# A graph network on one core: from one pair of graphs at a time to three stages with buffers of their own

## The chip, the core and the metric

One core of a Trainium2 chip. Times are device microseconds (us) of one whole execution, the median of several. "Clock" is the mean granted TensorE clock of an execution, 1.0 being full. A program on one core is compared in rounds with the kernel before on the same chip. In profile lines PE is TensorE (matrix products and transposes) and PEld its loads of weights; DVE is VectorE, ACT ScalarE and POOL GpSimd, which do the rest. SBUF is the memory that they work in, PSUM the one that takes TensorE's results, which the kernels hand out in tiles called banks (a wide tile counts as two).

## The reference, cut to what matters

64 graphs of 256 nodes with 256 features, fp32, with an integer adjacency matrix each. Four layers follow one another, and each ends with `x = layernorm(x + layer(x))`:

```
layer 0  masked attention, 8 heads of 32:  x1 = LN(x + softmax(mask(q k^T)) v Wo^T; ln1)
         feed-forward 256 -> 1024 -> 256:  x2 = LN(x1 + relu(x1 W1^T + b1) W2^T + b2; ln2)
layer 1  graph attention: h = x W^T, e = leaky(f_i + g_j), masked softmax, out = softmax(e) h + bias
layer 2  graph attention as before, then elu
layer 3  two convolutions: elu(x w_root + b + (mask^T x / degree) w_rel), twice
```

## The kernel before

It takes the graphs two at a time: 32 pairs, one after another. A pair has six norms: one after attention, two in a row after the feed-forward, one after each graph attention, one after the convolutions. Each norm goes from VectorE (statistics) to GpSimd (add epsilon, power of -0.5) and back to VectorE. The result of the power is called the root below. All big values share a few tags ("res", "xT") and the four PSUM banks of "mm":

```python
    ps_s = ctx.enter_context(tc.tile_pool(name="ps_s", bufs=2, space=PSUM))
    ps_m = ctx.enter_context(tc.tile_pool(name="ps_m", bufs=4, space=PSUM))
    ...
    def layer_norm(y, g=None, b=None):
        ...
        for i in range(NT):
            nc.vector.bn_stats(st[:, i, :], y[:, i, :])
            nc.vector.bn_aggr(mv[:, i, :], st[:, i, :])
        rstd = small.tile([P, NT], F32, tag="rstd", name="rstd")
        nc.gpsimd.tensor_scalar(rstd, mv[:, :, 1], EPS, None, op0=ALU.add)
        nc.gpsimd.tensor_tensor(rstd, rstd, neghalf, op=ALU.pow)
        o = tok(F32, "res", RES)
        for i in range(NT):
            mean, r = mv[:, i, 0:1], rstd[:, i : i + 1]
            if g is None:
                nc.vector.tensor_scalar(o[:, i, :], y[:, i, :], mean, r, op0=ALU.subtract, op1=ALU.mult)
            else:
                ...
        return o
    ...
    with tc.tile_pool(name="work", bufs=2) as pools["work"]:
        loaded = {0: load(x_view[0], adj_view[0])}
        for g in range(B // 2):
            ...
            xt = layer0(xt, attention(transposed(xt), am))
            xt = layer1(xt, gm)
            xt = layer2(xt, gm)
            xt = layer3(xt, adj)
            nc.sync.dma_start(out_view[g], xt)
```

## Time and profile before

| | before |
|---|---|
| median of 3 runs | 5842.55 us (5841.83 to 5842.78) |
| steady time of one pair | 180.9 us |
| TensorE busy, clock | 68%, 0.794 |
| VectorE, GpSimd, ScalarE busy | 45%, 21%, 18% |

The profile lines are shown in the prediction. One more view is used from here on, a **ledger of TensorE's time**, worked out from the trace. All matmul records of 16 steady pairs are sorted by their start. From one start to the next, the usual distance of that form at full clock is "work" (for example 0.429 us for 512 columns), time in which no record runs is "empty", and what remains is excess, booked by the clock at that moment. I read excess at full clock mostly as waiting that the record does not show as a gap. Before, a pair's 180.9 us are 90.3 of work, 56.9 empty, 27.3 of excess at half clock and 6.4 of excess at full clock.

### The profile page before, as it was taken

The numbers are of one execution on the slowest core, as the hardware profiler recorded it, in microseconds if no ns is written. First come the engines' busy times: TensorE is split into PE (matmuls) and PEld (weight loads), VectorE is DVE, ScalarE is ACT, GpSimd is POOL, SyncE is SP. The second block draws the span as 40 slices with busy tenths as digits, with TensorE's granted clock in tenths as the row PEclk, the third lists the DMA queues.
The fourth block names the chain that finished last, engine by engine and source line by source line (L and its number), as shares of the span: only waits on it lengthen the run. The fifth ranks groups of instructions, "written<-read, shape, count | busy, mean of one in ns | idle before, by whom it ended". The sixth has DMA issues, their size and how long they took to land. (4 is left out here: it accounts for less than half of the span.)

```text
span 5841.5 us, 44000 instructions
## 1 busy us (share of the span) xinstructions
PE 3973.4 (68%) x17170; PEld 2521.4 (43%) x17170; DVE 2625.8 (45%) x5370; ACT 1074.5 (18%) x1953; POOL 1255.0 (21%) x1012
## 2 busy tenths in 40 slices
PE   5766677666776667666677666777666776667766
PEld 3444444444444444444444444444444444444443
DVE  3444444544445434454444443444434445444453
ACT  1211112111121111111111211112111121111211
POOL 2221222212222122221122211222212222122221
PEclk8877788777887778877788777887777887778877
DMA  2000000000000000000000000000000000000000
GB/s 67 8 11 4 11 11 8 11 7 9 11 8 11 11 4 11 8 11 11 4 11 11 8 11 4 11 11 8 11 4 11 11 8 11 4 11 11 4 4 4
DMA packets 55542, 59.78 MB, mean 10 GB/s; under 512 B 2016, under 2 KB 54496, under 8 KB 55328
## 3 DMA queue, kind: packets, MB, share of 16 engines
q1 hardware_dynamic: 50688, 50.34, 2.8%
q10 hardware_dynamic: 4032, 5.24, 0.3%
q8 instruction: 137, 2.24, 0.2%
q0 software_dynamic: 608, 1.32, 0.1%
q14 instruction: 77, 0.63, 0.0%
HBM read 40.12 MB, written 16.78 MB: 10 GB/s over the span
## 5 line engine op out<-in xcount | busy, mean ns | idle before, releaser
L179 PE MATMUL mm<-ident,res 128*128 128x128 f32 x1280 | 331.9, 431 | 1123.5 <-DVE res L199 869.5
L179 PEld LDWEIGHTS mm<-ident,res 128*128 128x128 f32 x1280 | 237.6, 212 | 1205.7 <-issue 652.7
L379 PE MATMUL mm<-h,e 128*128 128x259 f32 x1024 | 418.0, 594 | 341.0 <-DVE e L371 341.0
L183 ACT COPY xT<-mm 128x512 f32<-128x512 f32 x192 | 112.3, 585 | 2504.2 <-PE mm L179 2504.2
L432 PE MATMUL mm<-cw,xT 128*128 128x512 f32 x1024 | 529.3, 675 | 4.6
L260 PE MATMUL mm<-xT,W1T 128*128 128x512 f32 x1024 | 496.7, 647 | 18.3 <-DVE xT L181 18.3
L244 DVE TENSOR_TENSOR res<-mm,res 128x512 f32<-128x512 f32 x128 | 86.5, 675 | 925.5 <-PE mm L242 925.5
L379 PEld LDWEIGHTS mm<-h,e 128*128 128x128 f32 x1024 | 313.0, 313 | 432.3 <-DVE e L371 353.2
L242 PE MATMUL mm<-W2T,hid 128*128 128x256 f32 x2048 | 447.2, 379 | 0.0
L242 PEld LDWEIGHTS mm<-W2T,hid 128*128 128x128 f32 x2048 | 389.1, 190 | 66.5 <-issue 15.3
L276 PE MATMUL mm<-gw,xT 128*128 128x258 f32 x1024 | 357.2, 523 | 23.0 <-DVE xT L181 18.3
L190 DVE BATCH_NORM_STATS2 st<-res 128x6 f32<-128x256 f32 x768 | 297.5, 412 | 159.3 <-POOL res L265 78.4
L338 ACT ACTIVATE p<-s 128x1024 f32<-128x1024 f32 x256 | 259.6, 1019 | 576.0 <-PE s L333 548.3
L333 PE MATMUL s<-qk 32*128 32x256 f32 x2048 | 286.3, 496 | 102.1 <-ACT p L338 64.5
L193 POOL TENSOR_SCALAR rstd<-mv 128x4 f32<-128x4 f32 x192 | 53.5, 279 | 1396.4 <-DVE mv L191 1396.4
L341 POOL TENSOR_TENSOR p<-p,am 128x1024 f32<-128x1024 f32 x128 | 305.2, 2384 | 202.5 <-ACT p L338 202.5
L432 PEld LDWEIGHTS mm<-cw,xT 128*128 128x128 f32 x1024 | 220.8, 223 | 283.5 <-issue 222.4
L352 DVE RECIPROCAL inv<-mm 128x512 f32<-128x512 f32 x64 | 214.9, 3358 | 273.5 <-PE mm L349 273.5
L260 PEld LDWEIGHTS mm<-xT,W1T 128*128 128x128 f32 x1024 | 212.9, 212 | 288.3 <-issue 257.3
L276 PEld LDWEIGHTS mm<-gw,xT 128*128 128x128 f32 x1024 | 272.6, 274 | 107.1 <-DVE xT L181 48.5
L199 DVE TENSOR_SCALAR res<-res,mv,rstd 128x256 f32<-128x256 f32 x512 | 239.7, 530 | 169.2 <-POOL rstd L194 167.8
L451 POOL TENSOR_TENSOR res<-res 128x1024 f32<-128x1024 f32 x32 | 75.1, 2347 | 1075.0 <-DVE res L296 1075.0
(112 smaller groups left out, 5858.8 us busy)
## 6 DMA issues: line engine op xcount, KB each, us to landing
x<-in_x_dram SPq DMA_DIRECT2D x32, 512.0 KB, 3.8
adj<-in_adj_dram SPq DMA_DIRECT2D x32, 512.0 KB, 3.8
out_dram<-res SPq DMA_DIRECT2D x32, 512.0 KB, 2.9
W1T<-in_W1T_dram ACTq DMA_DIRECT2D x1, 1024.0 KB, 8.6
W2T<-in_W2T_dram ACTq DMA_DIRECT2D x1, 1024.0 KB, 18.5
WqkvT<-in_WqkvT_dram ACTq DMA_DIRECT2D x1, 768.0 KB, 4.6
cw<-in_w_root_dram ACTq DMA_DIRECT2D x2, 256.0 KB, 8.4
cw<-in_w_rel_dram ACTq DMA_DIRECT2D x2, 256.0 KB, 8.7
```

The costliest lines, as they stand in the source:

```text
L179: nc.tensor.transpose(pt[:, i * P : (i + 1) * P], xt[:, i, kb * P : (kb + 1) * P], ident)
L190: nc.vector.bn_stats(st[:, i, :], y[:, i, :])
L199: nc.vector.tensor_scalar(o[:, i, :], y[:, i, :], mean, r, op0=ALU.subtract, op1=ALU.mult)
L242: nc.tensor.matmul(po[:, i, :], lhsT=lhs(c)[:, tile_i], rhs=rhs(c), start=(c == 0), stop=(c == n - 1))
L260: nc.tensor.matmul(ph, lhsT=w1[:, kb, f * P : (f + 1) * P], rhs=x1T[:, kb, :], start=(kb == 0), stop=(kb == KB - 1))
L276: nc.tensor.matmul(ph, lhsT=xT[:, kb, i * P : (i + 1) * P], rhs=w[:, kb, :], start=(kb == 0), stop=(kb == KB - 1))
L333: nc.tensor.matmul(s[r // 2][:, r % 2, hg, :], lhsT=qk[rows_r, KB + hg, n * P : (n + 1) * P], rhs=qk[rows_r, hg, queries], start=True, sto ...
L338: nc.scalar.activation(pu, s[u], AF.Exp, accum_out=sums[:, u : u + 1])
L341: eng.tensor_tensor(flat, flat, am[:, n, None, :].to_broadcast([P, 4, N]), op=ALU.mult)
L352: nc.vector.reciprocal(inv, pd)
L379: nc.tensor.matmul(po, lhsT=e[:, 2 * b + kt, i * P : (i + 1) * P], rhs=h[:, 2 * b + kt, :], start=(kt == 0), stop=(kt == 1))
L432: nc.tensor.matmul(po, lhsT=hT[:, kb, n * P : (n + 1) * P], rhs=w[:, kb, :], start=(kb == 0), stop=(kb == KB - 1))
```

## The change

The intent: three pairs under way at once. The work is cut into three stages (attention with its norm; feed-forward and first graph attention; second graph attention and convolutions), each with SBUF tags and PSUM banks of its own, so that the holes of one pair can take the matmuls of two others. To make room, norms and row biases work in place, and x and adj are loaded again where a later stage needs them. Some checks and a few passes were moved or merged. The core of the diff, cut:

```diff
-    ps_s = ctx.enter_context(tc.tile_pool(name="ps_s", bufs=2, space=PSUM))
-    ps_m = ctx.enter_context(tc.tile_pool(name="ps_m", bufs=4, space=PSUM))
+    ps = {
+        "wide": ctx.enter_context(tc.tile_pool(name="ps_wide", bufs=2, space=PSUM)),
+        "a": ctx.enter_context(tc.tile_pool(name="ps_a", bufs=2, space=PSUM)),
+        "b": ctx.enter_context(tc.tile_pool(name="ps_b", bufs=2, space=PSUM)),
+    }
...
+    s1, s2, s3, gen = Stage("a_", "wide"), Stage("b_", "a"), Stage("c_", "b"), Stage("g_", "a")
...
+    def add_row(xt, row):
+        nc.gpsimd.tensor_tensor(xt, xt, over_tiles(row), op=ALU.add)
...
-        o = tok(F32, "res", RES)
         for i in range(NT):
-            mean, r = mv[:, i, 0:1], rstd[:, i : i + 1]
+            yi, mean, r = y[:, i, :], mv[:, i, 0:1], rstd[:, i : i + 1]
             if g is None:
-                nc.vector.tensor_scalar(o[:, i, :], y[:, i, :], mean, r, op0=ALU.subtract, op1=ALU.mult)
+                nc.vector.tensor_scalar(yi, yi, mean, r, op0=ALU.subtract, op1=ALU.mult)
...
-        x2 = layer_norm(y, ln2g, ln2b)
-        nc.gpsimd.tensor_tensor(x2, x2, xt, op=ALU.add)
-        return layer_norm(x2)
+        layer_norm(st, y, ln2g, lambda i: xt[:, i, :])
+        layer_norm(st, y)
...
+    def stage1(g, kept):
+        xt, adj = kept.pop("in")
+        am, kept["gm"] = masks(s1, adj)
+        xT = transposed(s1, xt)
+        add_row(xt, bo)
+        kept["x"] = attention_end(s1, xt, attention(s1, xT, am, g))
+
+    def stage2(g, kept):
+        xt = load(s2, x_view[g], F32, "x")
+        kept["x"] = layer1(s2, feed_forward(s2, kept["x"], xt), kept["gm"], 2 * g)
+
+    def stage3(g, kept):
+        adj = load(s3, adj_view[g], I32, "adj")
+        xt = layer2(s3, kept["x"], kept["gm"], 2 * g + 1)
+        nc.sync.dma_start(out_view[g], layer3(s3, xt, *relation(s3, adj, g)))
...
+        for step in range(G + 2):
+            if step >= 2:
+                stage3(step - 2, pairs.pop(step - 2))
+            if 1 <= step <= G:
+                stage2(step - 1, pairs[step - 1])
+            if step + 1 < G:
+                fetch(step + 1)
+            if step < G:
+                stage1(step, pairs[step])
```

## The prediction

> **What bounds the kernel now.** I read the page's busy shares first, then the timeline of one pair of graphs, then a table of windows that cuts that pair into the stages the change uses.
>
> The page's first two parts (busy time and share by engine; the span in 40 slices):
>
> ```profile
> PE 3973.4 (68%) x17170; PEld 2521.4 (43%) x17170; DVE 2625.8 (45%) x5370; ACT 1074.5 (18%) x1953; POOL 1255.0 (21%) x1012
> ...
> PEclk8877788777887778877788777887777887778877
> DMA  2000000000000000000000000000000000000000
> ```
>
> No engine is full. TensorE is busiest, at 68%, and its granted clock is about 0.8 all along (mean 0.794). DMA is near zero after the first loads, so bandwidth is no limit. A kernel in which nothing is full waits on its own chain.
>
> The timeline of TensorE for one pair (start us, length us, line, in brackets the idle time before and its releaser):
>
> ```profile
> 2071.47 3.57 PE L242 MATMUL mm<-WoT,ctxT 128*128 128x256 f32 x8 [2.30 <-DVE ctxT L353]
> 2079.03 2.31 PE L179 MATMUL mm<-ident,res 128*128 128x128 f32 x8 [3.99 <-DVE res L202]
> 2081.91 15.49 PE L260 MATMUL mm<-xT,W1T 128*128 128x512 f32 x32 [0.57 <-DVE xT L181]
> 2097.23 13.98 PE L242 MATMUL mm<-W2T,hid 128*128 128x256 f32 x64
> 2122.90 2.19 PE L179 MATMUL mm<-ident,res 128*128 128x128 f32 x8 [11.69 <-DVE res L199]
> ...
> 2137.15 6.62 PE L379 MATMUL mm<-h,e 128*128 128x259 f32 x16 [5.32 <-DVE e L371]
> 2147.20 1.94 PE L179 MATMUL mm<-ident,res 128*128 128x128 f32 x8 [3.44 <-DVE res L199]
> ...
> 2161.33 6.47 PE L379 MATMUL mm<-h,e 128*128 128x259 f32 x16 [5.32 <-DVE e L371]
> 2167.64 0.34 PE L417 MATMUL mm<-ones_b,rel_b 128*128 128x1 bf16 x8
> 2180.10 2.10 PE L179 MATMUL mm<-ident,res 128*128 128x128 f32 x8 [12.11 <-DVE res L199]
> ```
>
> Every norm (L199, L202) and every softmax of the graph attention (L371) leaves TensorE empty for 3 to 12 us, and no matmul of another pair stands in these holes. The first matmuls of the next pair come only after the last convolution of this one: all pairs draw from the same tags (the four banks of "mm", "res", "xT"), and these are handed out in program order. So the period is one pair's latency: the second convolution's transposes start at 2015.27 and at 2196.14, 180.9 us apart, and 32 x 180.9 = 5788 leaves 53 us for start and end.
>
> The same pair by stage (attention; its output product and norm; feed-forward and first graph attention; second graph attention and the convolutions; last row, the whole period):
>
> ```profile
> core 0: us, PE busy (x) PEld busy (x) DVE busy (x) ACT busy (x) POOL busy (x), PEclk, DMA share, GB/s
> 2027.60:2071.40 43.80, 34.64 (x250) 19.18 (x248) 30.88 (x38) 11.39 (x20) 19.29 (x14) 0.88 0.08 25
> 2071.50:2079.00 7.50, 3.54 (x8) 2.50 (x9) 4.22 (x14) 0.00 (x0) 1.53 (x3) 0.73 0.00 0
> 2079.00:2147.10 68.10, 46.71 (x148) 31.46 (x148) 21.48 (x60) 10.04 (x17) 11.09 (x10) 0.80 0.03 8
> 2147.20:2208.60 61.40, 39.21 (x134) 25.66 (x135) 25.27 (x60) 12.11 (x24) 6.87 (x5) 0.73 0.00 1
> 2027.60:2208.40 180.80, 123.93 (x538) 78.71 (x536) 81.85 (x168) 33.54 (x61) 38.88 (x31) 0.79 0.03 9
> ```
>
> Of a period TensorE is busy 124 us and empty 57 us; VectorE is busy 82. The new stages are 51, 68 and 61 us long when alone.
>
> [...]
> - [...] Starts of 512-column matmuls (L260) are 429 ns apart where the granted clock is 1.0 and 853 ns where it is 0.5, and the transposes that follow the norms (L179 on res) nearly all run at 0.5, 214 ns apart, against 109 for the transposes of x, which follow a full stretch.
> - [...] the 128x256 norm step (L199) took 407 ns on average with GpSimd idle and 2440 ns in the 31 cases where it mostly lay beside a GpSimd instruction; the head mask (L341) took 1.22 us at least and 2.20 us beside GpSimd.
> - [...]
>
> **The change, part by part.**
>
> *Own buffers and banks for each stage (the main part).* Attention works in two 4 KB PSUM tiles, the other two stages in two banks each, and each has its own SBUF tags. The holes of one pair can then take matmuls of two others. TensorE's work at full clock, from the start-to-start times in the trace at clock 1.0, per pair: 48 fp32 transposes x 109 ns = 5.2; 8 bf16 ones x 56 and 8 broadcasts x 108 = 1.3; L218 16 x 429 = 6.9; L229 16 x 216 = 3.5; L333 in 16 groups of four at 232 = 3.7; L349 in 32 groups of four at 217 = 6.9; WoT 16 x 216 = 3.5; W1 32 x 429 = 13.7; W2 64 x 216 = 13.8; L276 32 x 217 = 6.9; L379 32 x 221 = 7.1; L432 32 x 429 = 13.7; L443 32 x 120 = 3.8; degrees 0.2. Sum **90 us**, against 124 busy today: the 34 us between are the half clock and the tails of bursts. If TensorE never idles, 32 pairs cost 2890 us.
>
> How full it gets: one chain alone at full clock has 90 us of TensorE and 57 us without it, so its idle share is 57/147 = 0.39. If three chains were idle independently, all three would be so 0.39^3 = 6% of the time: 96 us a pair. Counting only two as able to cover for each other (stages hand over to each other[...]) gives 15% idle: **106 us**. I choose the second, and add the next item.
>
> *More VectorE beside GpSimd.* GpSimd's long SBUF-reading instructions come to about 26 us per pair (six 128x1024 adds of 2.34 to 2.69, four mask products of 2.38, two of 1.27). [...] Some 47 VectorE instructions per pair can be caught, each for half of about 2.3 us: 47 x 0.23 x 1.15 = 12 us, of which I put half on the path: **6 us**. Together 112 us.
>
> *Operations removed from VectorE.* Bias of v folded into the output bias (L231, 1.3 us per pair, now a ScalarE copy of about 0.6 us x 2); the squares and maxima of the checks (L361, L362, 0.7) to GpSimd (about 0.44 x 2); three passes over "other" (L410 to L412, 2.1) become one of about 1.2; the fp32r compare (L406), 2.43 us beside GpSimd's compare (L408, 2.81 us, now gone), perhaps 0.7. Saved: 1.3 + 0.7 + 0.9 + 1.7, some 4.6 us, so VectorE falls from 82 to about 77 before new blocking, near 89 after it. GpSimd falls from 39 to about 35. None sets the period while TensorE needs 90.
>
> *Norms and biases in place.* The residual add between the two norms (L265, 2.34 us plus its 2.45 us wait) leaves the chain, since x + bias is made earlier. As chain time this is covered by other pairs anyway; what it buys is SBUF room.
>
> *Added:* x and adj are loaded once more, 1 MB per pair, at a DMA share of 0.03: hidden. *Start and end:* 53 us as now, then the first steps with one stage (51) and two (about 70), the last with two (75) and one (61): 310 us, around 30 full steps.
>
> Sum: 30 x 112.5 + 310 = 3685, **say 3690 us**.
>
> **Rivals.**
> 1. *VectorE becomes the bound.* 77 us of work plus 12 or more of blocking is as much as TensorE's 90[...]. For it: the 2440 ns case above. [...] It would give 120 to 130 us a pair: 3900 to 4200.
> 2. *Banks bind.* Attention had eight banks and gets four, of which scores take all four at once; a stage with two banks can run only one group ahead. For it: in the convolution ScalarE and VectorE need 0.37 + 0.43 + 0.41 us per bank after a 1.7 us product. Against: that is shorter than the product, and other stages fill in. If wrong, holes of 1 to 3 us return between groups, and the time goes to about 4000.
> 3. *Nearly perfect overlap.* 96 us a pair and a clock of 1.0: about 3190. For it: long FFN and convolution bursts need almost nothing from VectorE. Against: fixed order, and two engines at over 80% together.
> 4. *No overlap gained* (a shared resource still in program order): about 5700. The distinct tags speak against it.
>
> **Range and chances.** 3380 to 4150: from 102 us a pair (3370) to 128 (4150). Faster by over 2% 0.97, within 2% 0.02, slower 0.01.
>
> **What would show it.** Right: TensorE busy over 85% with the clock over 0.93; transposes after norms at some 110 ns instead of 214; the steady period 105 to 120 us; VectorE's and GpSimd's shares rising to about 70% and 30%; L199 and L202 longer on average than 530 and 482 ns. Wrong: a clock still near 0.8 (holes remain), VectorE over 85% busy (rival 1), or TensorE waiting chiefly for evacuations (rival 2).

## The result

| | before | after |
|---|---|---|
| median | 5842.59 us | 4516.38 us (4493.25 to 4520.36, 4 runs) |
| ratio | | 0.7722 (95% interval 0.77 to 0.7744) |
| steady time of one pair | 180.9 us | 136.7 us (one of 130 to 137, one of 138 to 143 in turn) |
| TensorE busy, clock | 68%, 0.794 | 84%, 0.877 |
| ledger: work / empty / half clock / full-clock excess | 90.3 / 56.9 / 27.3 / 6.4 | 91.0 / 19.9 / 15.9 / 10.0 |

Ratios, here and below, are the mean time of one kernel's runs over that of the other's runs of the same rounds, so not quite the ratio of the medians. Executions over 1.5% slower than the fastest of the same kernel are left out of the means. The change is a large gain, but 826 us short of the 3690 predicted, and outside the range.

The page of the changed kernel (busy time and share by engine; the clock in 40 slices, in tenths):

```profile
PE 3769.8 (84%) x17174; PEld 2277.5 (51%) x17174; DVE 2498.4 (56%) x5148; ACT 1097.4 (24%) x2017; POOL 1114.0 (25%) x915
...
PEclk8888889889898988888988898898888988899887
```

TensorE is fuller, VectorE is not: 56%, where about 70% was forecast. The clock rose only to 0.877. The table of windows shows how two successive pairs go through (four phases, then the whole double period):

```profile
core 0: us, PE busy (x) PEld busy (x) DVE busy (x) ACT busy (x) POOL busy (x), PEclk, DMA share, GB/s
2006.70:2050.50 43.80, 43.80 (x165) 27.91 (x164) 22.12 (x53) 10.64 (x19) 3.61 (x3) 1.00 0.12 36
2050.50:2132.70 82.20, 65.67 (x351) 39.06 (x350) 48.13 (x89) 21.13 (x41) 27.14 (x21) 0.83 0.04 13
2132.70:2186.70 54.00, 51.64 (x191) 32.03 (x190) 26.53 (x65) 13.55 (x23) 8.10 (x8) 0.97 0.06 20
2186.70:2273.00 86.30, 67.95 (x356) 40.75 (x355) 51.81 (x94) 21.70 (x41) 26.44 (x22) 0.82 0.06 19
2006.70:2280.90 274.20, 234.38 (x1070) 142.41 (x1069) 153.62 (x317) 67.61 (x125) 68.86 (x56) 0.87 0.06 20
```

The overlap is not even. In the short phases (44 and 54 us) the feed-forward of one pair and the convolutions of the pair before fill TensorE, at clock 1.00 and 0.97. In the long ones (82 and 86 us) the two graph attentions of a pair run beside the attention of the next, full of norms and softmaxes; TensorE is busy 80% and 79% of them, at clock 0.83 and 0.82. A pair takes from its attention's start at 2050.9 to the end of its convolutions near 2320, about 270 us: two periods, so on average two pairs are under way, not three.

Inside a long phase, holes stand ahead of the transposes that follow a norm (timeline of TensorE; start, length, in brackets the idle time before and what ended it):

```profile
2060.69 1.01 PE L227 MATMUL ps_a<-ident,b_x 128*128 128x128 f32 x4 [2.72 <-DVE b_x L247]
...
2085.79 1.12 PE L227 MATMUL ps_b<-ident,b_x 128*128 128x128 f32 x3 [4.23 <-DVE b_x L247]
...
2124.46 1.54 PE L227 MATMUL ps_a<-ident,a_x 128*128 128x128 f32 x6 [3.84 <-DVE a_x L250]
2126.78 3.82 PE L421 MATMUL ps_b<-c_h,c_e 128*128 128x259 f32 x8 [0.78 <-DVE c_e L413]
```

L247 and L250 are the last steps of norms. These holes stood there before too (35.2 us a pair ahead of such transposes, 3.8 of it behind an elu and not a norm; now 10.4); they shrank, but in a kernel with three stages one expects them filled. The clock shows it too: of the transposes that follow a norm 73% still start at half clock (before, 1272 of the 1280 transposes of res, L179, did), where the prediction's sign of being right was 110 ns instead of 214.

Two smaller forecasts can be checked at once in the groups by line, after:

```profile
L247 DVE TENSOR_SCALAR b_x<-b_x,b_mv,b_rstd 128x256 f32<-128x256 f32 x256 | 150.4, 649 | 113.2 <-POOL b_rstd L243 113.2
...
L247 DVE TENSOR_SCALAR c_x<-c_x,c_mv,c_rstd 128x256 f32<-128x256 f32 x128 | 44.2, 408 | 64.2 <-POOL c_rstd L243 64.2
...
L452 DVE TENSOR_SCALAR c_rel<-c_adj 128x1024 fp32r<-128x1024 int32 x32 | 21.8, 683 | 0.0
```

The same norm step takes 649 ns on average where it often lies beside a GpSimd instruction (45 of these 256 lie for over half their length beside one and take 1788 ns, 185 lie beside none and take 406 at the median), and 408 ns where it does not: the slowing beside GpSimd that the prediction had read from the kernel before (407 against 2440 ns for this step; "blocking" below) is there. Not every instruction shows it: in the kernel before, the copy L181 out of PSUM took 692 ns on average in the 64 cases beside a GpSimd instruction and 689 in the 128 others. The fp32r compare fell from 2428 to 683 ns, as predicted.

### The profile page after: what moved, and what is told of

It reads as the page before. It is cut to its first block, busy times and chain, and to the rows that moved or that the text cites. A ratio compares the mean times of both kernels' runs of the same rounds, so it can differ in the third digit from the quotient of the medians.

```text
span 4491.5 us, 44308 instructions
## 1 busy us (share of the span) xinstructions
PE 3769.8 (84%) x17174; PEld 2277.5 (51%) x17174; DVE 2498.4 (56%) x5148; ACT 1097.4 (24%) x2017; POOL 1114.0 (25%) x915
## 4 chain that ended last, share of the span: by engine, by line
PE 57%; DVE 22%; POOL 11%; ACT 5%; issue 3%; DVEq 0%; POOLq 0%; ACTq 0%
PE ps_b L477 10%; PE ps_a L304 7%; PE wide L393 6%; PE ps_a L282 6%; PE wide L377 4%; PE ps_b L227 4%; PE ps_b L487 3%; POOL a_p L386 3%; PE ps_a L421 3%; PE ps_a L320 3%; PE ps_b L421 3%; PE ps_b L320 2%; DVE a_inv L396 2%; DVE b_x L247 2%; PE wide L258 2%
## 5 line engine op out<-in xcount | busy, mean ns | idle before, releaser
L304 PE MATMUL ps_a<-b_xT,W1T 128*128 128x512 f32 x1024 | 514.5, 630 | 21.4 <-DVE b_xT L229 20.4
L477 PE MATMUL ps_b<-cw,c_xT 128*128 128x512 f32 x1024 | 459.9, 603 | 0.5 <-DVE c_xT L229 0.3
L282 PE MATMUL ps_a<-W2T,b_hid 128*128 128x256 f32 x2048 | 457.7, 379 | 0.0
L377 PE MATMUL wide<-a_qk 32*128 32x256 f32 x2048 | 374.3, 462 | 62.3 <-ACT a_p L383 58.1
L282 PEld LDWEIGHTS ps_a<-W2T,b_hid 128*128 128x128 f32 x2048 | 384.4, 190 | 63.3 <-issue 14.8
L383 ACT ACTIVATE a_p<-wide 128x1024 f32<-128x1024 f32 x256 | 261.4, 1023 | 564.5 <-PE wide L377 548.9
L386 POOL TENSOR_TENSOR a_p<-a_p,a_am 128x1024 f32<-128x1024 f32 x128 | 282.3, 2206 | 386.7 <-ACT a_p L383 384.8
L258 PE MATMUL wide<-a_xT,WqkvT 128*128 128x512 f32 x512 | 299.8, 727 | 77.2 <-DVE a_xT L229 76.4
L377 PEld LDWEIGHTS wide<-a_qk 32*128 32x128 f32 x2048 | 202.1, 211 | 208.0 <-ACT a_p L383 95.6
L393 PE MATMUL wide<-a_p,ones 128*32 128x256 f32 x2048 | 220.2, 490 | 24.5 <-POOL a_p L386 20.2
L393 PE MATMUL wide<-a_p,a_v 128*32 128x256 f32 x2048 | 221.5, 423 | 20.8 <-POOL a_p L386 18.5
L247 DVE TENSOR_SCALAR b_x<-b_x,b_mv,b_rstd 128x256 f32<-128x256 f32 x256 | 150.4, 649 | 113.2 <-POOL b_rstd L243 113.2
L421 PE MATMUL ps_b<-c_h,c_e 128*128 128x259 f32 x512 | 190.2, 522 | 16.7 <-DVE c_e L413 16.5
```

The source lines that it names most:

```text
L247: nc.vector.tensor_scalar(yi, yi, mean, r, op0=ALU.subtract, op1=ALU.mult)
L258: nc.tensor.matmul(pq, lhsT=wqkv[:, kb, c * P : (c + 1) * P], rhs=xT[:, kb, :], start=(kb == 0), stop=(kb == KB - 1))
L282: nc.tensor.matmul(po[:, i, :], lhsT=lhs(c)[:, tile_i], rhs=rhs(c), start=(c == 0), stop=(c == n - 1))
L304: nc.tensor.matmul(ph, lhsT=w1[:, kb, f * P : (f + 1) * P], rhs=x1T[:, kb, :], start=(kb == 0), stop=(kb == KB - 1))
L377: nc.tensor.matmul(s[r // 2][:, r % 2, hg, :], lhsT=qk[rows_r, KB + hg, n * P : (n + 1) * P], rhs=qk[rows_r, hg, queries], start=True, sto ...
L383: nc.scalar.activation(pu, s[u], AF.Exp, accum_out=seen_sum[:, k : k + 1])
```

## The experiments

**Which order or buffer holds the pairs up?** Four kernels change nothing but the order in which instructions are built or given priority, or the banks. (`high_priority(offset=n)` moves instructions n places forward in the order in which the builder of the program places them, a negative n back.)

e1 puts stage 1 ahead of the others:

```diff
-                stage1(step, pairs[step])
+                with tc.high_priority(offset=600):
+                    stage1(step, pairs[step])
```

> Edit: stage 1 (attention) of a step is given a higher scheduling priority than stages 3 and 2 of the same step; nothing else. Theory P (the order: oldest pair first, so feed-forward and convolutions take TensorE together at 100% for 44-54 us and attention, norms and graph attention are left for the remaining 82 us, where gaps and the half clock gather): the period falls from 137 us to 125 or less, the total from 4516 to about 4000-4200, with idle plus half-clock TensorE time per pair falling from 36 us to about 22. Rival B (buffers and banks: one x1 buffer and two wide PSUM tiles hold attention back): within 2% of the changed kernel, 4430-4610.

Measured: 4575.12 us, ratio 0.7838, 139.1 us a pair (91.0 work, 24.1 empty, 13.4 half clock, 10.6 full-clock excess).

e2 builds pair after pair, and leaves the overlap to the distinct tags alone:

```diff
-        for step in range(G + 2):
-            ...
+        for g in range(G):
+            if g + 1 < G:
+                fetch(g + 1)
+            stage1(g, pairs[g])
+            stage2(g, pairs[g])
+            stage3(g, pairs.pop(g))
```

> Edit: the program text runs pair by pair (stage 1, 2, 3 of pair g, then of pair g+1), not skewed by step. Theory P (own tags make the overlap, text order gives only priorities, and oldest-first is the same relation among pairs): within 2% of the changed kernel, 4430-4610. Rival (the skewed text itself makes the overlap): back towards the kernel before, over 5300.

Measured: 4685.69 us, ratio 0.8016, 144.4 us a pair (23.9 empty, 18.0 half clock).

e3 lets stages 2 and 3 share one pool of four banks in place of two each:

```diff
-        "a": ctx.enter_context(tc.tile_pool(name="ps_a", bufs=2, space=PSUM)),
-        "b": ctx.enter_context(tc.tile_pool(name="ps_b", bufs=2, space=PSUM)),
+        "a": ctx.enter_context(tc.tile_pool(name="ps_a", bufs=4, space=PSUM)),
...
-    s1, s2, s3, gen = Stage("a_", "wide"), Stage("b_", "a"), Stage("c_", "b"), Stage("g_", "a")
+    s1, s2, s3, gen = Stage("a_", "wide"), Stage("b_", "a"), Stage("c_", "a"), Stage("g_", "a")
```

> Edit: stages 2 and 3 draw from one pool of four PSUM banks under one tag in place of two pools of two. If tags are handed out in program order (my reading of the kernel before), stages 2 and 3 run one after the other: 68 + 61 us alone, so a period of at least some 145 us and a total of 4800-5300. If slots are handed out as they come free, the four banks are more flexible than two and two: 4350-4520.

Measured: 4546.68 us, ratio 0.778, 138.2 us a pair (23.7 empty, 14.1 half clock). In its trace the feed-forward starts only after the second convolution of the pair before, and it costs 0.7%. Banks of their own for stages 2 and 3 buy next to nothing. The times of e2 and e3 lie in neither of their expected ranges.

e6 lowers the feed-forward's priority:

```diff
         hid = []
+        low = tc.high_priority(offset=-600)
+        low.__enter__()
         ...
         y = product_plus(st, "x2", ...)
+        low.__exit__(None, None, None)
```

> Edit: the feed-forward products (L304, L306 and the second product) are put 600 places back in priority, about one step, so that they fill what others leave. Theory P: the 28 us of feed-forward move into the gaps of attention and norms; period 125 us or less, total 3950-4200, granted clock over 0.92. Rival B: within 2% of 4516. A miss in the other direction is possible: the feed-forward is on the longest chain, and if it is delayed too far the period grows over 140 us (over 4600).

Measured: 4776.89 us, ratio 0.8179, 146.8 us a pair.

My theory that the fixed order of stages alone cost the missing time found no support: four arrangements give 138 to 147 us a pair, all slower, with 24 us empty each. Rival B (buffers and banks hold attention back) expected e1 where it came, but was not tested: no run gave attention more than two wide PSUM tiles, or any stage a second copy of its SBUF values. A fifth, e10, moves stage 1 only between the other two, with `offset=180` where e1 has 600:

> Stage 1 (attention) is given an earlier place in TensorE's order by a set number of steps, so that it goes ahead of stage 2 and behind stage 3, and is no longer held back while feed-forward and convolutions fill TensorE. Theory L: if attention is spread over the period instead of lying beside the two graph attentions alone, both of a pair's chains overlap better; 2 to 4% less than the changed kernel, 4340 to 4430 us. If another single loop takes over at once, as in the two orders tried before: 4516 to 4700 us.

Measured: 4901.73 us, ratio 0.8387, 150.2 us a pair, of it 21.8 of excess at full clock, twice that of the changed kernel. It missed both expectations.

**Is it the half clock?** e5 puts filler matmuls behind each norm's statistics, ahead of the transposes that wait for the norm:

```diff
+            if kb == 0 and fill is not None:
+                for i in range(NT):
+                    nc.tensor.matmul(pt[:, 0:256], lhsT=ident, rhs=fill[:, i, 0:1].to_broadcast([P, 256]),
+                                     start=True, stop=True)
             for i in range(NT):
                 nc.tensor.transpose(pt[:, i * P : (i + 1) * P], xt[:, i, kb * P : (kb + 1) * P], ident)
...
+        if st is not gen:
+            fills[id(y)] = mv
```

> Filler matmuls (full-width fp32, 256 columns) are put on TensorE behind each norm's statistics, ahead of the transposes that wait for that norm[...]. They add about 4 x 0.22 us of work per norm of the feed-forward and graph layers, some 4.4 us per pair. Theory C (the half clock itself costs the missing time: 15.8 us a pair in the ledger of the changed kernel): the granted clock rises above 0.93 and the period falls from 137 to 125 us or less, about 4100 to 4200 us. Theory L (the chains of two pairs set the period, and the half clock is mostly a symptom of the gaps they leave): [...] the time moves by less than 3%, between 4400 and 4600 us.

Measured: 4370.0 us, ratio 0.7478 (0.7465 to 0.749), right result, the fastest right kernel of all. The page:

```profile
PE 3809.2 (87%) x18206; PEld 2347.7 (54%) x18206; DVE 2456.2 (56%) x5148; ACT 1107.4 (25%) x2017; POOL 1098.1 (25%) x915
...
PEclk8999989999999999999999999999999999999997
```

The clock is 0.943, and the ledger's half-clock excess falls from 15.9 to 5.5 us a pair. But the period falls only from 136.7 to 133.1, which fits neither theory whole: work rises by 7.0 (the fillers: 16 a pair, each two records that at full clock start 0.217 us apart; 4.4 had been expected), empty time falls from 19.9 to 15.5, and full-clock excess rises from 10.0 to 14.1. So of 10.4 us taken from the half clock 3.6 came back as time. How much of the rest went to the fillers' own work, and how much is the old waiting, now spent at full clock, this run cannot tell. That the half clock is largely a symptom of the waits is suggested more plainly by e18 below, where it falls to 6.0 without a filler.

**Is it the length of the norms' waits?** e8 adds three powers by one, so the same result, to each norm:

```diff
         nc.gpsimd.tensor_tensor(rstd, rstd, neghalf, op=ALU.pow)
+        for _ in range(3):
+            nc.gpsimd.tensor_tensor(rstd, rstd, plusone, op=ALU.pow)
```

> Three more powers (by one, so the result is the same) follow each norm's power on GpSimd: 18 instructions of 1.04 us per pair, 18.7 us, on an engine that is busy 25% of the time, and no other work anywhere. Theory L (a pair's chain of 272 us, two pairs under way at a time, sets the period): the period grows by about 18.7/1.98 = 9.4 us, to 146.5, and the time by 6 to 7%, about 4810 us. A rival, theory T (the period is set by how much TensorE gets through, with its clock): the added waits are filled by other pairs and the time stays within 2% of the changed kernel, 4430 to 4600 us.

Measured: 5178.51 us, ratio 0.8862, 158.7 us a pair: 22.0 more for 18.7 added (later expectations say 20.7, the growth of the whole time shared over 32 pairs). That is neither theory. The chain that ended last, by engine for the changed kernel and then by engine and by line for e8:

```profile
PE 57%; DVE 22%; POOL 11%; ACT 5%; issue 3%; DVEq 0%; POOLq 0%; ACTq 0%
```

```profile
PE 48%; POOL 21%; DVE 20%; ACT 4%; issue 3%; POOLq 0%; DVEq 0%; ACTq 0%
PE ps_b L480 9%; PE ps_a L307 6%; POOL b_rstd L246 6%; PE wide L396 5%; PE wide L380 4%; POOL c_rstd L246 4%; PE ps_a L424 3%; PE ps_b L228 3%; PE ps_b L424 3%; DVE b_x L250 3%; PE ps_b L490 2%; PE ps_a L323 2%; POOL a_p L389 2%; DVE a_inv L399 2%; POOL b_rstd L244 2%
```

L246 is the added power: at least 10% of the span, some 520 us or 16 us a pair, lies on the chain that sets the end. GpSimd, busy 33% of the time, holds 21% of that chain. How one wait holds more than its own pair shows in the timeline of e8 (all engines; a is the stage-1 pair, b stage 2, c stage 3):

```profile
2119.26 1.06 ACT L415 ACTIVATE c_e<-c_e 128x1024 f32<-128x1024 f32 x1 [0.81 <-DVE c_e L414]
...
2121.06 3.18 POOL L246 TENSOR_TENSOR a_rstd<-a_rstd,plusone 128x4 f32<-128x4 f32 x3
2124.27 1.67 DVE L253 SCALAR_TENSOR_TENSOR a_x<-a_x,a_rstd,row_ln_b 128x256 f32<-128x256 f32 x4 [4.19 <-POOL a_rstd L246]
2124.82 1.97 PE L228 MATMUL ps_a<-ident,a_x 128*128 128x128 f32 x8 [7.18 <-DVE a_x L253]
2125.86 1.22 DVE L416 TENSOR_TENSOR c_e<-c_e,a_gm 128x1024 f32<-128x1024 f32 x1
...
2127.14 1.23 PE L424 MATMUL ps_b<-c_h,c_e 128*128 128x259 f32 x2 [0.35 <-DVE c_e L416]
```

Pair c's exponential is done at 2120.3. Its mask step (L416) is VectorE's, and VectorE stands idle for 4.19 us at L253, which waits for pair a's root, and takes L416 only behind it. So L416 runs at 2125.86, 5.5 us late, and c's products (L424) come behind it: two pairs wait for one norm.

e19 adds one power instead of three (its diff is against e8), and e18 takes the root away: every norm multiplies by a constant 0.5 (a wrong result).

```diff
-        for _ in range(3):
+        for _ in range(1):
```

> One more power in each norm instead of three: 6.2 us a pair of added wait. If paid in full from the first microsecond: 6.2 to 7 us of the period, about 4730 us. If part of it is covered: 4530 to 4640 us.

```diff
-        rstd = st.small([P, NT], "rstd")
-        nc.gpsimd.tensor_scalar(rstd, mv[:, :, 1], EPS, None, op0=ALU.add)
-        nc.gpsimd.tensor_tensor(rstd, rstd, neghalf, op=ALU.pow)
+        rstd = plushalf
```

> A wrong result on purpose: every norm multiplies by a constant 0.5 instead of its root, so the two GpSimd instructions and VectorE's wait for them (1.5 to 2.2 us in each of six norms, some 11 us a pair) are gone, and nothing else. If every microsecond of that wait is paid, as the three added powers were: 11 to 12 us a pair less, about 4130 us. If the order of the changed kernel already covers a wait of this length and only more than that is paid: within 3% of it, 4380 to 4560 us.

Measured: e19 4751.49 us, ratio 0.813. e18 4025.59 us, ratio 0.689 (0.6878 to 0.6901), relative error 0.76. The page of e18:

```profile
PE 3550.2 (88%) x17174; PEld 2198.6 (55%) x17174; DVE 2374.6 (59%) x5149; ACT 1106.9 (28%) x2017; POOL 861.9 (21%) x531
...
PEclk9999989999999998999999999998999989999997
```

"Wait" is the time from the last statistic of a norm to its first step that uses the root, summed over a pair's six norms, from the trace:

| | wait | period | work | empty | half clock | full-clock excess | clock |
|---|---|---|---|---|---|---|---|
| e18, no root | -9.7 | 121.6 | 91.0 | 11.9 | 6.0 | 12.7 | 0.941 |
| after | 11.4 | 136.7 | 91.0 | 19.9 | 15.9 | 10.0 | 0.877 |
| e19, one power more | 18.0 | 145.1 | 91.0 | 25.4 | 19.4 | 9.3 | 0.851 |
| e8, three more | 29.7 | 158.7 | 91.0 | 39.7 | 19.5 | 8.6 | 0.823 |

From the changed kernel to e19 and on to e8, each microsecond of wait costs 1.25 and 1.17 us of the period (the curve, below). No part of the added wait is covered by the other pairs. Of e8's 19.8 us more of empty time, 19.2 stand directly ahead of transposes that follow a norm (10.4 to 29.6 us). TensorE's order of matmuls over four pairs is 99% (e19) and 98% (e8) that of the changed kernel, VectorE's order 96% and 95%, so little else moved.

e18 does not lie on this curve, for it takes away more than the wait. Its first step no longer waits for the statistics of all four tiles of a pair, as a root for all four made it do (VectorE, e18):

```profile
2030.43 0.16 DVE L241 BATCH_NORM_AGGREGATE c_mv<-c_st 128x2 f32<-128x6 f32 x1
2030.51 1.90 DVE L246 TENSOR_SCALAR c_x<-c_x,c_mv,plushalf 128x256 f32<-128x256 f32 x1
2032.34 0.17 DVE L241 BATCH_NORM_AGGREGATE c_mv<-c_st 128x2 f32<-128x6 f32 x1
```

L246 is the first step, the second L241 the last statistic of the same norm; hence the wait below zero. From the last statistic to the end of the last step, a pair's norms take 25.0 us in the changed kernel and 7.1 in e18: 17.9 us less, which bought 15.1 us of the period, more than either expectation of e18. These 15.1 are 8.0 of empty time and 9.9 of half clock, less 2.7 at full clock, so a good half came through the clock. But TensorE's order is 89% that of the changed kernel and VectorE's 78%; e18 bounds what the norms cost no better than that.

Nor does the wait alone set the period where the order changes: e1 has a wait of 17.3 us and a period of 139.1, e17 (below) 9.7 and 138.2.

**Is VectorE short of time?** e13 gives it work that nothing waits for, eight statistics of a constant in each norm:

```diff
+        junk = st.small([P, nc.vector.BN_STATS_DIM], "junk")
+        for _ in range(8):
+            nc.vector.bn_stats(junk, ln1g)
```

> Eight statistics of 0.4 us over a constant are put on VectorE in each of a pair's six norms: 19 us a pair of work that nothing waits for, on an engine that is busy 56% of the time; no wait and no chain is made longer by itself. Theory Q (a stalled or occupied VectorE queue holds all pairs): about as dear as the slow norms, 10 to 20 us a pair, 4830 to 5150 us. Theory L or a bound by TensorE: it goes into VectorE's idle 44%, under 3%, 4450 to 4640 us.

Measured: 4551.64 us, ratio 0.7776. The builder put all of this work into the first 1461 us, which makes a better test than the one planned: windows of 550 us with it and without it, in one execution,

```profile
500.00:1050.00 550.00, 466.15 (x2138) 282.90 (x2138) 475.00 (x1184) 138.11 (x252) 138.34 (x112) 0.88 0.06 20
2000.00:2550.00 550.00, 470.38 (x2137) 286.00 (x2136) 311.87 (x640) 135.91 (x250) 136.34 (x112) 0.87 0.06 20
```

VectorE (third busy time) is 86% busy in the first and 57% in the second. Two pairs take 276.5 us in both. VectorE has room to spare; that what counts is instead what it stands waiting for is a reading, and the next runs do not all bear it out.

**Can the wait be moved or cut?** Eight kernels.

e9 takes the root on ScalarE:

```diff
-        nc.gpsimd.tensor_scalar(rstd, mv[:, :, 1], EPS, None, op0=ALU.add)
-        nc.gpsimd.tensor_tensor(rstd, rstd, neghalf, op=ALU.pow)
+        nc.scalar.activation(rstd, mv[:, :, 1], AF.Ln, bias=epsc)
+        nc.scalar.activation(rstd, rstd, AF.Exp, scale=-0.5)
```

> The opposite: each norm's root is taken on ScalarE as exp(-0.5 ln(var + eps)) instead of an add and a power on GpSimd (0.28 + 1.04 us)[...]. If no tables have to be changed between the two functions, theory L expects about 6 x 0.9 = 5.4 us less per pair's chain, some 2.7 us of the period, 2% of the time: about 4430 us. Theory T expects no change. If tables are changed for it, the time rises, and the profile shows ScalarE's table loads.

Measured: 4626.73 us, ratio 0.7935. ScalarE's groups show why:

```profile
L243 ACT ACT_TABLE_LOAD x192 | 246.3, 1283 | 3.4
```

The tables are loaded twice in each norm (192 times at L243 and 192 at L244), 1283 ns each time. The two functions themselves take 297 and 205 ns; the 0.9 us that a norm was to save was my estimate, with a time for ScalarE that no trace had shown. The wait grew to 14.9 us a pair and the period to 140.3, near the curve's 141.

e12 leaves the root and moves the last step of the four norms without gain to ScalarE:

```diff
             if g is None:
-                nc.vector.tensor_scalar(yi, yi, mean, r, op0=ALU.subtract, op1=ALU.mult)
+                nc.scalar.activation(yi, yi, AF.Identity, bias=shift[:, i : i + 1], scale=r)
```

(`shift` is minus the mean times the root; VectorE makes the sign and GpSimd the product.)

> The slow-norm run cost 20.7 us a pair for 18.7 us of added GpSimd time, and VectorE's waits for the root grew from 9.3 to 27.2 us a pair. New theory Q (queues): [...] while VectorE stands at one pair's normalisation and waits for GpSimd, the evacuations of the two other pairs that lie behind it stand too; a wait on one pair's chain is then paid by all three. Here the last step of four of the six norms of a pair (subtract mean, multiply) goes to ScalarE (24% busy), with a scale and a bias per token; each norm's own chain gets longer by one GpSimd multiply (about 0.3 us) and not shorter otherwise. Theory Q: VectorE's waits at those norms (220 us in all, 6.9 a pair) go, with some 7 us of work; the period falls by 5 to 12 us, 4130 to 4360 us. Theory L (length of the chain alone): the time rises by 1% or so, 4520 to 4600 us.

Measured: 4515.15 us, ratio 0.7728, the same as the changed kernel. VectorE's standing for the root fell from 9.3 to 2.5 us a pair, and nothing came of it: the wait itself, now in front of ScalarE's queue, is 12.3 us instead of 11.4, and the period 137.4.

e14 is e5 and e12 together:

> The filler matmuls and the normalisation on ScalarE together. If they are separate gains they add: 3.2% and what the run with ScalarE alone gives, about 4000 to 4250 us and the fastest of all; if they fill the same holes, no better than the better of the two alone (4370 us or so).

Measured: 4486.03 us, ratio 0.7676. The gains do not add; the wait is 14.7 us against e5's 11.9, and the period 136.5 against 133.1.

e17 moves each normalisation 60 places back in priority and changes nothing else:

```diff
-        for i in range(NT):
-            yi, mean, r = y[:, i, :], mv[:, i, 0:1], rstd[:, i : i + 1]
-            ...
+        with tc.high_priority(offset=-60):
+            for i in range(NT):
+                yi, mean, r = y[:, i, :], mv[:, i, 0:1], rstd[:, i : i + 1]
+                ...
```

> The changed kernel with each normalisation (the instructions that wait for the root) put back in the order by 60 places of priority, so that VectorE's ready work of other pairs goes ahead of it; no instruction added, removed or made faster. Theory F (ready work stands behind a waiting instruction in the fixed order): VectorE's waits for the root fall from 9.3 us a pair to below 5 and the time to 4300 to 4430 us. If nothing else is ready then: no change, 4470 to 4560 us.

Measured: 4532.55 us, ratio 0.7758. VectorE's standing fell only to 6.9 us a pair, and the time not at all. Priority did not get ready work past the wait.

e15 takes the root on VectorE itself, with an integer first guess and two Newton steps:

```diff
+        bits = rstd.bitcast(I32)
+        nc.vector.tensor_scalar(var, mv[:, :, 1], EPS, None, op0=ALU.add)
+        nc.vector.tensor_scalar(bits, var.bitcast(I32), 1, None, op0=ALU.logical_shift_right)
+        nc.vector.tensor_scalar(bits, bits, -1, 0x5F3759DF, op0=ALU.mult, op1=ALU.add)
+        for _ in range(2):
+            nc.vector.tensor_tensor(step, var, rstd, op=ALU.mult)
+            nc.vector.scalar_tensor_tensor(step, step, -0.5, rstd, op0=ALU.mult, op1=ALU.mult)
+            nc.vector.scalar_tensor_tensor(rstd, step, 1.5, rstd, op0=ALU.add, op1=ALU.mult)
```

> Each norm's root is taken on VectorE (an integer first guess and two Newton steps, nine instructions on 128x4 values [...]) in place of the two GpSimd instructions (0.3 + 1.04 us, with a semaphore each way, some 1.9 us from the last statistic to the first normalised tile). Theory W (what a norm waits is paid one to one, 20.7/18.7 = 1.1): 6 x 1.1 us x 1.1 = 7 us a pair less, period 130, time about 4290 us. If the wait counts only where it is long, or VectorE's own work has become the bound: within 1% of 4516 us or slower.

Measured: 4440.49 us, ratio 0.76 (0.7587 to 0.7613), right result. It gained, but less than one expectation and more than the other. The 1.1 us that a norm was to save was my estimate, with a time for the small steps that came from no trace; the kernel before already took 162 and 178 ns for its two VectorE instructions on 128x4 values (L420, L421). Here nine small steps that need one another start 0.2 us apart, and steps of other pairs lie between them, so the time from statistic to first use did not shrink, it doubled, to 22.9 us a pair. The curve would make that 150 us; the period is 134.9. The difference to the right kernels so far: VectorE's waits for a root are gone, and it serves other pairs meanwhile. That fits the timeline of e8 above, but e15's order of matmuls is only 88% that of the changed kernel, so this one run does not prove it.

e16 is e15 with e5's filler:

> The same with the filler matmuls that keep TensorE's clock up (4370 us by themselves). If the two gains add: about 4150 us, clock 0.94 or more, the fastest of all runs. If both only filled the same holes ahead of the transposes: about 4370 us.

Measured: 4540.14 us, ratio 0.7774, slower than either alone. The half clock came back (13.4 us against 5.5).

Last, a small cut that keeps the result right: e20 moves only the addition of epsilon to VectorE, and e21 does so with the filler.

```diff
-        nc.gpsimd.tensor_scalar(rstd, mv[:, :, 1], EPS, None, op0=ALU.add)
+        nc.vector.tensor_scalar(rstd, mv[:, :, 1], EPS, None, op0=ALU.add)
```

> The addition of epsilon in each norm goes from GpSimd (0.28 us and its start) to VectorE, which has just made the variance; the power stays on GpSimd. The wait of a norm falls by some 0.25 us, 1.5 us a pair; at the rate of the curve (1.2 to 1.3 us for each) that is 1.9 us a pair, 60 us of the time: about 4455 us. If the new order of instructions that the edit brings outweighs it: anything within 3% of 4516 us.

> The same with the filler matmuls (4370 us alone). If both add: about 4310 us and the fastest right kernel. If the new order outweighs it, as it did with the root on VectorE and the filler together: 4350 to 4550 us.

Measured: e20 4549.24 us, ratio 0.7787; e21 4405.21 us, ratio 0.7535. No gain: e20 is 0.8% slower than the changed kernel, and in its trace the wait is 11.5 us and so not smaller at all, though VectorE stands for the root 7.1 us a pair instead of 9.3; e21 is 0.8% slower than e5. These differences are clear of the noise (the intervals are some 0.2% to either side), but of the other sign than the saving of some 60 us that was expected of e20. Why is not shown.

## Why the prediction was wrong, point by point

**What held.** Faster by over 2%, for the reason given: the holes of one pair take matmuls of others, and empty time fell from 56.9 to 19.9 us a pair. TensorE's work is 91.0 us where 90 was added up. The empty time was forecast at 16 (106 less 90) and 6 for blocking, 22 together; 19.9 were found. Rival 1 (VectorE as the bound) is refuted by e13, and rivals 3 and 4 did not come. Of rival 2 (banks) e3 tests only what stages 2 and 3 have; attention's four banks in place of eight were not varied. Its scores (L377) account for 1.8 us a pair of empty time and 4.4 of excess at full clock, so TensorE did not wait chiefly there.

**What failed: the step that put TensorE's work into the sum at full clock.** The prediction had seen 34 us a pair between the work and the busy time, "the half clock and the tails of bursts", and dropped them: the sum 30 x 112.5 has no term for them, and the text expected the clock over 0.93, where it came to 0.877. Left are 15.9 us at half clock (27.3 before) and 10.0 of excess at full clock (6.4 before; now above all in the scores of the attention, 4.4 us). With them 112.5 + 1.0 - 2.6 + 25.9 = 136.8, and 136.7 was measured. Over 30 steps that is 726 us; start and end took 415 us (4516 less 30 x 136.7) instead of 310. Together that is the 831 us from the sum's 3685 to 4516.

**Behind it: the model of independent chains.** "If three chains were idle independently" and "Counting only two as able to cover" gave an idle share near the one measured, so the ledger's empty column looks like a success. It is luck at least in part, for the model answers wrongly when a wait changes. Add e8's 18.7 us to its 57 of 147, and the square of the idle share goes from 0.15 to 0.21 and the pair from 106 to 114 us: 8 more. The chip took 22 more. Take e18's 17.9 us away, and the model gives 7 less; the chip gave 15.1 less, with another order of instructions. The pairs do not cover what is added to each other's norms. As an estimate from e18, 15.1 less 7, so some 8 of the 24.2 us by which a pair missed the forecast, would be norms that the model thought covered; this cuts across the terms above and does not add to them. The other 16 are not taken apart here.

**Smaller steps.** VectorE was to rise to about 70% and GpSimd to 30%; they are at 56% and 25%, because the period is longer, and because the blocking hardly grew: VectorE's time over the median of the same instruction with no GpSimd instruction beside it (the shortest, where none stood alone) is some 5.7 us a pair, and was 5.4 before, where 12 more had been added up (an estimate from the trace before: 47 instructions, times the 23% that GpSimd's 26 us make of 112, times 1.15). The steps that came from L199 did get longer (588 against 530 ns over all of them), those from L202 did not (478 against 482). Loads stayed hidden, as said (DMA share 0.06 over a double period). Of the times estimated for moved and merged instructions, the copy of v (L271 on ScalarE) takes 586 ns where 600 were written and the merged pass (L454 on VectorE) 1218 where 1200 were; the checks' step (L404 on GpSimd) takes 203 to 290 where 440 were.

**What stays open.** Whether it is the standing queue or the length of the dependent chain that costs 1.2 to 1.3 us for each one: e8's timeline and e15 speak for the queue, e12 and e17 give it no support, and no run separates them at one fixed order of instructions. Open too: what more PSUM for attention or a second SBUF copy for a stage would give, and why e10 doubles the full-clock excess.

## What to carry to other kernels

When several chains share an engine on which a ready step of one stands behind a wait of another (5.5 us on VectorE in e8), do not multiply their idle shares. Lengthen one wait on purpose by a known amount and see what part of it comes back: here all of it did, which showed in one run that the overlap did not cover that wait. Add the clock's loss as a term of its own; but before paying for it with filler, ask whether it is the cause or the trace of the same waits, and count the filler's own work (here 7.0 us of filler took 10.4 from the half clock and 3.6 came back, still the best right kernel, 3.2% faster).

## What else the traces show

- Half clock after small gaps: of the changed kernel's 131 drops to half clock after the first 200 us, 115 had no TensorE gap over 3.41 us in the 8 us before them; in the last 3.41 us before a drop TensorE was busy 32% of the time at the median. In e18 it is 76 of 80, and 38%. In both a drop mostly comes after several small gaps and not after one long one. (3.41 us is taken from the traces: 135 of the changed kernel's 136 half-clock stretches last 1 to 5 times that, 82 of e18's 83 last 1, 2, 3 or 5 times that.)
- The program built for e9 loaded ScalarE's tables 384 times for 192 pairs of logarithm and exponential, at 1283 ns each; the changed kernel loads a table once.
- Here 18.7 us a pair on GpSimd, 25% busy, cost 22.0 us, and VectorE could go from 57% to 86% busy for nothing. Occupancy alone does not show this; what ends TensorE's gaps does (19.2 us of e8's 19.8 more stand directly ahead of transposes that follow a norm).
- A power on GpSimd takes 1.04 us for 128x4 values; VectorE instructions on 128x4 values that need one another are 0.2 us from start to start in e15.
